# A mixture's first tiles and the attention behind it: routing products, registers, rotary tables and the order of keys

## The chip, the core and the metric

The kernel runs on one core of a Trainium2 chip. A core has five engines with a queue of instructions each: TensorE (PE in the profile, with its weight loads as PEld), VectorE (DVE), ScalarE (ACT), GpSimd (POOL) and SyncE (SP). SP computes nothing; in this kernel it issues most of the transfers between the device memory and the on-chip memory. The metric is the device time of one execution in microseconds, less being better.

## The reference

Four layers, each with an attention and a feed-forward part, on `x` of 4 x 256 tokens with 256 features, and a context of 4 x 1601 tokens. Every part sees a layer norm of `x` and adds its result to `x`. Two parts matter here.

The first feed-forward part is a mixture of eight experts. Each token goes to its two best experts; an expert is three products with biases, with an exact GELU after the first two.

```
gate_weights = softmax(x @ Wg + bg)
topv, topi   = top_k(gate_weights, 2)
h  = gelu(x @ W1[e] + b1[e])
h  = gelu(h @ W2[e] + b2[e])
eo = h @ W3[e] + b3[e]
out = sum over e of comb[.., e] * eo[e]      # comb: topv at topi, 0 elsewhere
```

The attention after it has 16 query heads and 4 heads of keys and values with 128 features. Its keys come from the context and from `x` itself (1601 + 256 = 1857 tokens); queries and keys are normalised by their root mean square and rotated by their positions (cosine and sine of position times frequency).

## The kernel before

The program is one function of some 2,400 lines; its stages follow one another on the one core. A planner of the language sets the order of the instructions within each engine's queue, and places the waits between engines. Inside a block `tc.manual_schedule(engines=...)` the engines named keep the order of the code; the others are still ordered by the planner.

*Routing the first mixture.* The first attention (`topk_attention`) routes three of the four batches beside its own work; the last batch's routing is left as a list of functions, `r["last"]`. It normalises two tiles of `x` (L626 on), multiplies by the gate (L654), finds the two best experts on DVE (L661 to L711), and writes each token's row by an indirect transfer from POOL to a table `XS` in device memory (L727), where each expert has its own range of rows.

*The mixture* (`sparse_moe`, PE, ACT and DVE in the order of the code, POOL and SP by the planner). `more_tiles` turns the counts of tokens into a list of 15 more tiles beyond the first tile of each of the eight experts: for each of the 15 the first row in `XS` and the place of its expert's weights, as whole numbers in `ix`. Whoever addresses memory by these numbers has to load them into registers of its engine (L812, `registers`). In the kernel before, all fifteen are loaded at once on SP (rows), PE and DVE (weights), directly after `ix`, and ahead of the rest:

```
rows = registers(ET.SP, 0, E * ROOM)
at_pe = registers(ET.PE, 1, (E - 1) * 4096)
at_dve = registers(ET.DVE, 1, (E - 1) * 4096)
```

Then come the biases of the 15 tiles (L837, L841: a product and a sum on DVE for each of two layers), and the third layer's biases, which are weighted by `comb` and added to `x` before the tiles (`cT`: transposes L847, copy L848, products L851, `residual` L853 with its sum on L181); `x` then goes to a table `XD` (L854), to which the tiles' results are added. The experts' weights `W` are eight transfers of 2 MB (L801): three at the start, five after the first four row fetches (L824).

The tile loop (L924 on) runs over 23 tiles in a software pipeline. A turn `t` fetches the rows of tile t+4, transposes the rows of tile t+1 (`turn`, L862, L864), does the first product of tile t and the second of tile t-1 (`layer`, L884 with GELU on L891), and the third of tile t-2 (`last`, L903), whose result is scaled (L905) and added to `XD` by an indirect transfer from POOL (L906). For a tile beyond the eighth DVE first copies the expert's weights of the first two layers from a place given by a register (`weights`, L874). The third product reads its weights through a PE register.

Beside the tiles the loop makes the rotary tables of the next attention: `rope_tables` is a generator, and `next(angles, None)` once per turn, from t = 1, does one step. Its first call loads the norm weights `rt_nw` (L953) and multiplies them on DVE (L954). For each of four batches it loads positions (L994), yields, converts them (L997), and does five steps of angles on DVE (L959 to L972), sine on ACT (L1003), products on POOL and DVE (L984 to L988) and a store into the table in device memory (L989). What is left after the loop runs then. At last SP loads `x` back from `XD` (L945).

*The next attention* (`gqa`, PE, ACT, DVE and POOL in the order of the code) gets `layernorm()` of all eight tiles of `x`, done before it starts (statistics L138 and L139, scaling L145, transposes L155). It works in units of one batch and one head of keys. Work is put into numbered slots with phases (`at(slot, phase, function)`). The first unit's queries and keys are made in slots -13 to -5 in ten groups, two a slot: groups 0 and 1 are queries, group 2 the keys of the batch's own `x`, groups 3 to 9 the context's keys. A group takes five slots: product (L1113 or L1187), norm (L1121 or L1194, with powers on POOL at L122) and scaling (L1129 or L1204) in the next one, rotation (L1160 on POOL, L1161 and L1162 on DVE), transposes, copy out. From slot -4 the scores (L1244) run. Weights of a unit come by three transfers (L1058, L1059); the first two units' are issued before the slots. Context and table pieces (`cx`, `tab`) are fetched three slots ahead (L1101, L1104).

Of the kernel before, what the change touches and what calls it, by code (L numbers as in the profile page):

```python
# [12 lines left out]
F32 = mybir.dt.float32  # L13
# [5 lines left out]
P = 128  # L19
B = 4  # L20
# [7 lines left out]
E = 8  # L28
# [24 lines left out]
def kernel(ctx: ExitStack, tc: tile.TileContext, A, out: bass.AP):  # L53
# [730 lines left out]
    def sparse_moe(r, k, XS, XD, tabs):  # L784
        ET = mybir.EngineType
        NT = E + MORE
        with (
# [15 lines left out]

            load(range(3))
            angles = rope_tables(one, tabs)
            for f in r["last"]:
                f()

            ix, ex, oh, _ = more_tiles(one, k, r["cum"], 4096.0)

            def registers(engine, which, top):
                return nc.values_load_multi_w_load_instructions(  # L812
                    ix[0:1, which, :], engines=[engine], min_val=0, max_val=top,
                    skip_runtime_bounds_check_because="made from counts of tokens that add up to twice their number",
                )[1]

            tiles = [{} for _ in range(NT)]

            def place(t, T):
                return T[t * ROOM : t * ROOM + P, :] if t < E else T[bass.ds(rows[t - E], P), :]  # L820

            def fetch(t):
                x = pool.tile([P, ROW], F32, tag="xs", name="xs", bufs=5)
                nc.sync.dma_start(x, place(t, XS))  # L824
                tiles[t]["x"] = x

            for t in range(4):
                fetch(t)
            load(range(3, E))
            rows = registers(ET.SP, 0, E * ROOM)  # L830
            at_pe = registers(ET.PE, 1, (E - 1) * 4096)
            at_dve = registers(ET.DVE, 1, (E - 1) * 4096)
            bias = one.tile([P, 2, MORE, 4], F32, tag="d_b", name="d_b")
            for layer in range(2):
                t4 = pool.tile([P, 1024], F32, tag="wd1024", name="d_t4", bufs=1)[:, 0 : MORE * 4 * E]
                t4 = t4.rearrange("p (d c e) -> p d c e", d=MORE, c=4)
                nc.vector.tensor_tensor(  # L837
                    t4, oh.unsqueeze(2).to_broadcast([P, MORE, 4, E]),
                    b12[:, layer].rearrange("p e c -> p c e").unsqueeze(1).to_broadcast([P, MORE, 4, E]), ALU.mult,
                )  # L840
                nc.vector.tensor_reduce(bias[:, layer], t4, AX.X, ALU.add)  # L841

            for h in range(2):
                cT = one.tile([E, 4 * P], F32, tag="cT", name="cT")
                tr = ps_tr()
                for q in range(4):
                    nc.tensor.transpose(tr[0:E, q * P : (q + 1) * P], r["comb"][:, h * 4 + q, :], ident)  # L847
                nc.scalar.copy(cT, tr[0:E, :])  # L848
                for q in range(4):
                    ps = ps_acc()  # L850
                    nc.tensor.matmul(ps[:, 0:D], cT[:, q * P : (q + 1) * P], b3, start=True, stop=True)  # L851
                    j = h * 4 + q
                    residual(j, ps[:, 0:D])  # L853
                    nc.sync.dma_start(XD[j * P : (j + 1) * P, :], X[j])  # L854

            first = one.tile([P, MORE], F32, tag="d_first", name="d_first")
            nc.vector.tensor_scalar(first, ex, -1.0 / 4096.0, float(E), ALU.mult, ALU.add)
# [9 lines left out]
            def weights(t, n):  # L867

                o, size = ((0, 1024), (1024, 2048))[n]
                if t < E:  # L870
                    w = W[:, t * 4096 + o : t * 4096 + o + size]
                else:
                    w = pool.tile([P, size], F32, tag=f"wd{size}", name=f"wd{size}", bufs=n + 1)
                    nc.vector.tensor_copy(w, W[:, bass.ds(at_dve[t - E] + o, size)])  # L874
                tiles[t]["w", n] = w.rearrange("p (c h) -> p c h", h=512)

            def layer(t, n):
# [15 lines left out]

            def last(t):
                v = tiles[t]
                ps = ps_acc()
                for q in range(4):
                    if t < E:
                        o = t * 4096 + 3072 + q * D
                        w3 = W[:, o : o + D]  # L900
                    else:
                        w3 = W[:, bass.ds(at_pe[t - E] + (3072 + q * D), D)]
                    nc.tensor.matmul(ps[:, 0:D], v["h"][:, q, :], w3, start=(q == 0), stop=(q == 3))  # L903
                y = pool.tile([P, D], F32, tag="y", name="y", bufs=3)
                nc.vector.tensor_scalar(y, ps[:, 0:D], v["g"], 1.0, ALU.mult, ALU.mult)  # L905
                nc.gpsimd.indirect_dma_start(  # L906
                    XD[:, :], bass.IndirectOffsetOnAxis(ap=v["to"], axis=0), y, None, compute_op=ALU.add
                )
# [15 lines left out]
            for t in range(NT + 2):  # L924
                if t + 4 < NT:
                    fetch(t + 4)
                if t + 1 < NT:
                    turn(t + 1)
                if t < NT:
                    layer(t, 0)  # L930
                if t >= 2:
                    last(t - 2)
                if t < NT:
                    weigh(t)
                    weights(t, 1)
                if t + 1 < NT:
                    weights(t + 1, 0)
                if 1 <= t <= NT:
                    layer(t - 1, 1)
                if t >= 1:  # L940
                    next(angles, None)
            for _ in angles:
                pass
            for j in range(NJ):
                nc.sync.dma_start(X[j], XD[j * P : (j + 1) * P, :])  # L945


    def rope_tables(pool, tabs):
# [39 lines left out]
                        nc.vector.scalar_tensor_tensor(tab[:, :, 1, hs], sin[:, 0:m], -1.0, wb[1], ALU.mult, ALU.mult)  # L988
                nc.sync.dma_start(tabs[b][:, at : at + m], tab)  # L989

        waiting = []
        for b in range(B):
            pi = pool.tile([P, nch], I32, tag="pos_i", name="pos_i", bufs=2)
            nc.sync.dma_start(pi, A["pos"][b])  # L994
            pf = pool.tile([P, nch], F32, tag="pos_f", name="pos_f", bufs=2)
            yield
            nc.vector.tensor_copy(pf, pi)  # L997
            for c0 in range(0, nch, 3):
                m = min(3, nch - c0)
                waiting.append((b, c0, m, *angle(b, c0, m, pf)))  # L1000
                yield
                for v in waiting[-1][3:]:
                    nc.scalar.activation(v, v, AF.Sin)  # L1003
                if len(waiting) > 1:
                    products(*waiting.pop(0))
        products(*waiting.pop(0))

    def gqa(xT, key, tabs=None, early=None, others=None):
# [14 lines left out]
        with (  # L1023
# [326 lines left out]

                others(at, lambda b: 4 * (16 * b + 15) + 13)
            weights(0)
            weights(1)
            for u in range(units):
                made = -(-loaded(u) // 2)
                n = len(pairs) - made + 2
                t0 = 16 * (u - 1) - 4 if u else -13
                if made:
                    load_keys(u, t0)
                if u > 1:  # L1360
                    at(t0 - 3, "early", lambda u=u: weights(u))
                for g in range(n):
                    t = t0 + (g // 2 if u == 0 else g * 12 // n)
                    if g < 2:
                        produce_queries(u, g, t)
                    else:
                        produce_keys(u, made + g - 2, t)
# [932 lines left out]
        with rings(0, x=0, tr=3, acc=5):  # L2300
            sparse_moe(r, k, XS, XD, tabs)
    with rings(0, sc0=1, sc1=1, sc2=1, tr=4, acc=1):
        gqa(layernorm(), "l1a", tabs)
    with rings(1):
        linear(layernorm())
    with rings(0, sc=3, tr=1, acc=1):
# [97 lines left out]
```

## Time and profile before

| what | value |
|---|---|
| median of 3 runs | 3754.8 us (3753.04 to 3756.34) |
| the profiled execution's own time | 3761.75 us |
| its span from the first to the last instruction | 3760.0 us |
| TensorE busy, share of the span | 3557.2 us, 95% |
| VectorE, ScalarE, GpSimd busy | 70%, 45%, 35% |
| mean granted TensorE clock | 0.970 |
| first mixture, from the statistics of its last routing to its last product | about 288.7 to 505.1 us |
| first scores of the next attention | 569.35 us |

The profile is one execution, 1.75 us longer than its span and 6.95 us above the median. "PE" rows are matrix products, "PEld" the weight loads that overlap them; rows with a small "q" (SPq, PEldq) are of an engine's sequencer, such as the issue of a transfer or the load of a register. A row of the timeline gives the start, the duration, engine, line, operation, what is written and read, and a count. The chain lists, back from the last instruction, what each step had waited for; "issue" in it is time in which the profile shows no wait. A row of the waits gives who waited, for whom, the total, how often and the longest.

### The profile page before, as it was taken

The page shows a single profiled execution, that of the slowest core. Times are in us where ns is not written, and L with a number is a line of the kernel's source. Part 1 is how long each engine was busy: PE and PEld are TensorE (multiplying, and loading weights), DVE is VectorE, ACT ScalarE, POOL GpSimd, SP SyncE. Part 2 cuts the span into 40 slices and gives each one's busy share as a digit, 9 for nine tenths or more (in the row PEclk, how much of TensorE's full clock was granted, in tenths as well). Part 3 has the DMA queues.
Part 4 walks back from the last instruction along what each step waited for, and adds up shares of the span by engine and source line. Part 5 has one row for each costly group of instructions (what it writes and reads, how often), then busy time and mean ns, then how long its engine had stood idle before and what let it go on. Part 6 is the DMA issues. An engine that isn't in the chain of part 4 may idle for free.

```text
span 3760.0 us, 63083 instructions
## 1 busy us (share of the span) xinstructions
PE 3557.2 (95%) x23397; PEld 2128.8 (57%) x23397; DVE 2615.3 (70%) x5204; ACT 1678.3 (45%) x4926; POOL 1311.5 (35%) x2091
## 2 busy tenths in 40 slices
PE   8887968999999999999999999987999999999998
PEld 4556954555555555555545555553555556556655
DVE  7894856777777777777667676525778766666664
ACT  4442645445444444444224444522444445545532
POOL 3332444444544544444321101012333433333332
PEclk9997989999999999999989999988999999999999
DMA  7326342222221222220100000033111111111103
GB/s 245 102 69 235 85 142 69 63 67 63 73 70 56 59 68 64 65 73 17 40 36 19 1 19 1 1 136 133 42 57 43 57 35 43 56 35 38 28 27 111
DMA packets 173715, 248.50 MB, mean 66 GB/s; under 512 B 21581, under 2 KB 134881, under 8 KB 169825
## 3 DMA queue, kind: packets, MB, share of 16 engines
q1 hardware_dynamic: 167025, 233.00, 19.9%
q0 software_dynamic: 6384, 11.47, 1.4%
q8 instruction: 186, 3.05, 0.3%
q14 instruction: 120, 0.98, 0.1%
HBM read 199.39 MB, written 45.03 MB: 65 GB/s over the span
## 4 chain that ended last, share of the span: by engine, by line
PE 70%; DVE 14%; POOL 7%; issue 5%; ACT 2%; DMA 2%; SPq 0%; another core or an unknown queue 0%; POOLq 0%; DVEq 0%; ACTq 0%
PE acc L1324 17%; PE sc L1244 15%; PE tr L1113 5%; PE sc L1657 4%; PE acc L1676 3%; PE tr L1187 3%; PE sc L1605 3%; DVE PT L1298 3%; POOL pe L1293 3%; PE acc L884 3%; POOL t L1160 2%; PE tr L1553 2%; PE tr L1337 2%; DVE m L521 2%; DVE work L523 1%
## 5 line engine op out<-in xcount | busy, mean ns | idle before, releaser
L1253 ACT ACTIVATE pe<-sc,ms 128x480 f32<-128x480 f32 (+1 forms) x1024 | 643.5, 631 | 892.7 <-DVE ms L1252 862.6
L1324 PE MATMUL acc<-PT,V 128*128 128x256 f32 (+1 forms) x3584 | 895.9, 390 | 6.9 <-ACT OT L1331 6.9
L1244 PE MATMUL sc<-KT,QT 128*32 128x480 f32 (+5 forms) x8192 | 883.1, 535 | 15.4 <-ACT pe L1253 12.1
L1293 POOL TENSOR_SCALAR pe<-pe,fac 128x480 f32<-128x480 f32 (+1 forms) x1024 | 654.8, 659 | 586.2 <-ACT pe L1253 213.7
L1324 PEld LDWEIGHTS acc<-PT,V 128*128 128x128 f32 (+1 forms) x3584 | 641.8, 190 | 349.4 <-issue 206.5
L1252 DVE TENSOR_REDUCE ms<-sc 128x1 f32<-128x480 f32 (+1 forms) x1024 | 607.9, 615 | 139.9 <-PE sc L1244 119.9
L1298 DVE STREAM_TRANSPOSE PT<-pe 128x1920 f32<-128x1920 f32 (+1 forms) x256 | 519.5, 2030 | 0.0
L1244 PEld LDWEIGHTS sc<-KT,QT 128*32 128x32 f32 x8192 | 220.9, 109 | 402.1 <-issue 321.8
L122 POOL TENSOR_TENSOR rs<-rsq_t,mhalf 128x2 f32<-128x2 f32 (+2 forms) x248 | 160.2, 646 | 568.6 <-DVE rsq_t L121 563.9
L1663 ACT ACTIVATE pt<-sc 128x1024 f32<-128x1024 f32 (+1 forms) x224 | 215.5, 962 | 280.7 <-PE sc L1657 245.9
L1113 PE MATMUL tr<-w,cx 128*128 128x256 f32 (+1 forms) x1264 | 303.5, 382 | 1.3 <-ACT nk L1129 1.3
L1619 DVE TENSOR_REDUCE mx<-sc 128x2 f32<-128x982 f32 (+2 forms) x224 | 211.6, 957 | 98.9 <-PE sc L1605 65.8
L1113 PEld LDWEIGHTS tr<-w,cx 128*128 128x128 f32 (+1 forms) x1264 | 226.7, 187 | 31.6 <-ACT nk L1129 2.0
L1657 PE MATMUL sc<-QT,KT 32*128 32x256 f32 (+1 forms) x1664 | 240.4, 403 | 0.0
L1605 PE MATMUL sc<-KT,QT 32*128 32x491 f32 (+4 forms) x1024 | 236.9, 564 | 0.0
L1253 ACT ACTIVATION_READ_ACCUMULATOR pe<-sc,ms 128x1 f32 x1024 | 199.4, 195 | 0.0
L1657 PEld LDWEIGHTS sc<-QT,KT 32*128 32x128 f32 (+1 forms) x1664 | 139.2, 182 | 92.8 <-issue 72.9
L1121 ACT ACTIVATE sq<-tr 128x128 f32<-128x128 f32 (+1 forms) x348 | 96.8, 278 | 171.5 <-PE tr L1113 166.4
L122 POOL TENSOR_TENSOR rsq<-rsq_t,mhalf 128x4 f32<-128x4 f32 x64 | 65.2, 1018 | 308.5 <-DVE rsq_t L121 308.5
L1676 PE MATMUL acc<-pt,vbuf 128*32 128x256 f32 (+1 forms) x1792 | 142.5, 391 | 0.0
L1161 DVE TENSOR_TENSOR nk<-nk,tab 128x256 f32<-128x256 f32 (+1 forms) x128 | 65.6, 513 | 100.2 <-POOL t L1160 99.0
L1187 PE MATMUL tr<-w,xlnT 128*128 128x512 f32 x256 | 126.1, 618 | 3.8 <-DMA wo<-in_l1a_wo 3.1
(430 smaller groups left out, 4774.5 us busy)
## 6 DMA issues: line engine op xcount, KB each, us to landing
cx<-in_ctxT SPq DMA_DIRECT2D x144, 256.0 KB, 3.0
tab<-rope SPq DMA_DIRECT2D x112, 256.0 KB, 2.7
w<-in_l0f_w SPq DMA_DIRECT2D x8, 2048.0 KB, 19.8
ctxT<-in_ctxT SPq DMA_DIRECT2D x7, 1601.0 KB, 6.5
w<-in_l2f_w SPq DMA_DIRECT2D x8, 1088.0 KB, 8.2
w<-in_l1a_wq SPq DMA_DIRECT2D x16, 512.0 KB
wo<-in_l1a_wo SPq DMA_DIRECT2D x16, 512.0 KB, 4.8
w<-in_l3a_wq SPq DMA_DIRECT2D x16, 512.0 KB, 7.3
```

The lines of the kernel that those rows point to most:

```text
L122: nc.gpsimd.tensor_tensor(dst, t[:n, :k], mhalf[:n, :k], ALU.pow)
L1113: nc.tensor.matmul(v["ps"][:n, i, :], lhs, st["wkv"][:, c, :], start=(c == 0), stop=(c == NC_ - 1))
L1187: nc.tensor.matmul(v["ps"], xtok(xT, b * 2 + tt, c), state[u]["wq"][:, c, :], start=(c == 0), stop=(c == NC_ - 1))
L1244: nc.tensor.matmul(sc[32 * r : 32 * r + 32, 0 : lens[r]], st["QT"][:, tt, o : o + 32], st["KT"][:, r, 0 : lens[r]], start=True, stop=True,)
L1252: nc.vector.tensor_reduce(top, sc, AX.X, ALU.max, negate=True)
L1253: nc.scalar.activation(w, sc, AF.Exp, bias=top, accum_out=s)
L1293: nc.gpsimd.tensor_scalar(w, w, v["fac"][:, g * 4 + a : g * 4 + a + 1], 1.0, ALU.mult, ALU.mult)
L1298: nc.vector.transpose(state[steps[i]][:, :, g * P : (g + 1) * P].rearrange("p k (a t) -> p a k t", a=4), pes[g].rearrange("p a (k i) -> p ...
L1324: nc.tensor.matmul(v["ps"][:, 0 : 2 * P], V[:n, k, :], PT[:n, k, :], start=(k == 0), stop=(k == nch - 1))
L1605: nc.tensor.matmul(st[:, j, c : c + n], QT[r, g, tt * P : (tt + 1) * P], KT[r, g, o : o + n], start=True, stop=True,)
L1657: nc.tensor.matmul(st[:n, j, q, :], KT[r, g, o : o + n], QT[r, :], start=True, stop=True)
L1676: nc.tensor.matmul(acc[32 * j : 32 * j + 32, a, :], V[:n, place, h * VW : h * VW + 32], pt[:n, j, q, :], start=(k == 0), stop=(k == nch - ...
```

## The change

In the mixture:

- `next(angles)` is called once ahead of `r["last"]`. The generator now loads all four position tiles, each into a buffer of its own, before its first yield, and does not yield again for each batch; twenty angle steps and the rest after the last one remain for the loop.
- Registers are loaded one by one: on SP where a tile's rows are fetched, on DVE where a tile's weights are first copied, on PE for tiles 8 to 15 ahead of the loop and for the others in `last`.
- The third layer's biases (`cT`) come directly after `more_tiles`; the first four row fetches stand after their first half, the last five weight transfers after their second half.
- The biases of the 15 tiles become a function that is called in turns 2 and 3.
- `x` is loaded back by transfers that ACT issues, no longer SP.

In the next attention:

- The layer norm is not finished before: its four pairs of tiles are put into slots, the first at -13 to -11, the others from -9, -8 and -7 on.
- The ten groups of the first unit come in the order 3, 4, 5, 6, 0, 1, 2, 7, 8, 9.
- The second unit's weights are issued in slot -12.

```diff
             load(range(3))
             angles = rope_tables(one, tabs)
+            next(angles)
             for f in r["last"]:
                 f()
 
             ix, ex, oh, _ = more_tiles(one, k, r["cum"], 4096.0)
 
-            def registers(engine, which, top):
+            def register(engine, which, i, top):
                 return nc.values_load_multi_w_load_instructions(
-                    ix[0:1, which, :], engines=[engine], min_val=0, max_val=top,
+                    ix[0:1, which, i : i + 1], engines=[engine], min_val=0, max_val=top,
...
             def place(t, T):
-                return T[t * ROOM : t * ROOM + P, :] if t < E else T[bass.ds(rows[t - E], P), :]
+                if t < E:
+                    return T[t * ROOM : t * ROOM + P, :]
+                return T[bass.ds(register(ET.SP, 0, t - E, E * ROOM), P), :]
...
-            for t in range(4):
-                fetch(t)
-            load(range(3, E))
-            rows = registers(ET.SP, 0, E * ROOM)
-            at_pe = registers(ET.PE, 1, (E - 1) * 4096)
-            at_dve = registers(ET.DVE, 1, (E - 1) * 4096)
-            bias = one.tile([P, 2, MORE, 4], F32, tag="d_b", name="d_b")
-            for layer in range(2):
...
                     residual(j, ps[:, 0:D])
                     nc.sync.dma_start(XD[j * P : (j + 1) * P, :], X[j])
+                if h == 0:
+                    for t in range(4):
+                        fetch(t)
+            load(range(3, E))
+            for t in range(E, E + 8):
+                tiles[t]["pe"] = register(ET.PE, 1, t - E, (E - 1) * 4096)
+            bias = one.tile([P, 2, MORE, 4], F32, tag="d_b", name="d_b")
+
+            def biases(layer):
...
-                    nc.vector.tensor_copy(w, W[:, bass.ds(at_dve[t - E] + o, size)])
+                    if n == 0:
+                        tiles[t]["dve"] = register(ET.DVE, 1, t - E, (E - 1) * 4096)
+                    nc.vector.tensor_copy(w, W[:, bass.ds(tiles[t]["dve"] + o, size)])
...
                 v = tiles[t]
+                if t >= E + 8:
+                    v["pe"] = register(ET.PE, 1, t - E, (E - 1) * 4096)
...
+                if t in (2, 3):
+                    biases(t - 2)
                 if t >= 1:
                     next(angles, None)
             for _ in angles:
                 pass
             for j in range(NJ):
-                nc.sync.dma_start(X[j], XD[j * P : (j + 1) * P, :])
+                nc.scalar.dma_start(X[j], XD[j * P : (j + 1) * P, :])
...
-        waiting = []
+        waiting, where = [], []
         for b in range(B):
-            pi = pool.tile([P, nch], I32, tag="pos_i", name="pos_i", bufs=2)
-            nc.sync.dma_start(pi, A["pos"][b])
+            where.append(pool.tile([P, nch], I32, tag=f"pos{b}", name="pos", bufs=1))
+            nc.sync.dma_start(where[b], A["pos"][b])
+        yield
+        for b in range(B):
             pf = pool.tile([P, nch], F32, tag="pos_f", name="pos_f", bufs=2)
-            yield
-            nc.vector.tensor_copy(pf, pi)
+            nc.vector.tensor_copy(pf, where[b])
...
             weights(0)
-            weights(1)
+            at(-12, "early", lambda: weights(1))
...
-                for g in range(n):
-                    t = t0 + (g // 2 if u == 0 else g * 12 // n)
+
+                order = [3, 4, 5, 6, 0, 1, 2, *range(7, n)] if rope and u == 0 else range(n)
+                for x, g in enumerate(order):
+                    t = t0 + (x // 2 if u == 0 else x * 12 // n)
...
-        gqa(layernorm(), "l1a", tabs)
+        xT, pairs = normed()
+
+        def norms(at, done):
+            for p, t in zip(pairs, (-13, -9, -8, -7)):
+                for f, slot, phase in zip(p, (t, t + 1, t + 2), ("early" if t == -13 else "late", "pe", "early")):
+                    at(slot, phase, f)
+
+        gqa(xT, "l1a", tabs, others=norms)
```

## The prediction

> **What bounds the kernel now.** First the page: TensorE (PE) fills the span as a whole, so a gain has to come from a stretch where it does not.
>
> ```profile
> span 3760.0 us, 63083 instructions
> PE 3557.2 (95%) x23397; PEld 2128.8 (57%) x23397; DVE 2615.3 (70%) x5204; ACT 1678.3 (45%) x4926; POOL 1311.5 (35%) x2091
> ```
>
> Then the chain in order of time, from 270 to 400 us and from 470 to 660 us. The diff touches two such stretches: the head of the first mixture, and the way from it into the next attention.
>
> ```profile
> 299.10 0.43 PE acc L742 x2
> 299.53 9.31 issue
> 308.84 1.02 PE tr L847 x4
> ...
> 314.80 25.98 DMA xd<-x
> ...
> 341.76 3.16 DMA rt_nw<-in_l1a_nw
> ...
> 345.56 3.68 PE acc L884 x16
> ```
> ```profile
> 519.26 2.29 DMA rope<-rt
> ...
> 523.01 5.51 DMA wo<-in_l1a_wo
> 528.55 6.05 PE tr L1187 x8
> ...
> 569.35 3.52 PE sc L1244 x13
> ```
>
> Then the waits of 293 to 350 us (who, for whom, total, times, longest): PE's two gaps at the head, and VectorE (DVE) held by one small load.
>
> ```profile
> PE tr L847 <- issue: 9.3, 1, 9.3
> PE tr L862 <- DMA xs<-xs: 5.9, 1, 5.9
> ```
> ```profile
> DVE rt_nw L954 <- DMA rt_nw<-in_l1a_nw: 19.0, 1, 19.0
> ```
>
> The DMA queue's own waits and SyncE's (SP's) rows say why: stores behind the 2 MB weight pieces wait up to 4.9 us for each piece.
>
> ```profile
> SPq L854 <- DMA w<-in_l0f_w: 22.6, 5, 4.9
> ```
> ```profile
> 288.65 0.33 SPq L797 DMA_DIRECT2D b<-in_l0f_b  x1
> 288.67 0.43 DVE L626 BATCH_NORM_STATS2 bnst<-x 128x6 f32<-128x256 f32 x1
> 289.02 1.29 SPq L801 DMA_DIRECT2D w<-in_l0f_w  x3
> ```
>
> Last, what a register load costs: fifteen at once 4.3 us on PE (the 9.3 gap ends with it), one alone 0.30.
>
> ```profile
> L2184 PEldq TENSOR_LOAD <-d_ix x15: 296/301/446, 3698.6 to 3720.9; - x15
> L812 PEldq TENSOR_LOAD <-d_ix x1: 4272/4272/4272, 304.5 to 304.5; - x1
> ```
>
> **The change part by part.** Times are against this execution (3761.75 us for a span of 3760.0; it lies 6.95 above the median of the runs, 3754.8). + is later.
>
> *Head.* (a) `next(angles)` now stands ahead of the last batch's routing, and it does more than issue loads: it multiplies `rt_nw` on DVE (L954), and DVE keeps program order, as the 19.0 us wait shows. Its load comes after three weight pieces on SP. The pieces, issued at 289.02, land about 4.9 us apart (the trace has 296.7, 301.6, 307.2; the last was slowed by row scatters), so the load behind them lands near 307. Its consumer then takes 0.23, and the statistics start at 307.3 instead of 288.67: **+18.6** on everything up to the tiles (routing, scatters, expert products). The four position loads are small and wait for nobody. (b) The products of L847 and L851 no longer wait for registers: the gap of **-9.3** goes. Late next are the residuals on DVE, which follow the routing arithmetic within the products' 10.9 us. (c) Eight single loads before the first tile: 8 x 0.30 = **+2.4** on PE (0 if its sequencer runs ahead, as the later mixture's rows do; I take all). DVE's fifteen ran beside PE's and go; fifteen single ones of 0.28 lie under the 1.2 us copy before each. The seven other PE loads lie under matmuls, as those of L2184 do, and SP's fifteen (0.28 each, four tiles ahead) under 7.3 us tiles: 0, or at worst 7 x 0.3 = 2.1 exposed. Tile 0 thus moves from 319.70 to 331.4. (d) The second stall: `turn(4)` could have run at 337.84 and the next tile at 345.15 (later transposes of L862 start 7.31 apart); it ran at 354.37, for rows behind weights, DVE held by `rt_nw`, and a clock of 0.5 afterwards. With SP idle for 18 us more, the remaining five pieces, which wait for no data, should be brought ahead, as the planner brought three position loads ahead at 342 to 347. Then rows of tile 4 are there when PE wants them (349.5): **-9.2**. Sum here +2.5.
>
> *Tile loop.* The twenty angle steps move from tiles 2 to 24, with four pauses, to tiles 1 to 20 without one; thirteen lie on tiles with weight copies in both. DVE is then nearly full: bursts of five end with periods of 7.91, 7.50 and 7.48 against 7.31. Without pauses I add **+1.2** (0 to 5). The biases (2 x 1.64 on DVE at tiles 2 and 3) lie beside 7.3 us of PE, where DVE is busy 4 to 5.7; without that cover +3.3. In the last tiles ACT no longer swaps tables for Sin (1.28 each) before Gelu: from the last `turn` at 480.67 PE took 24.4 us, of which 22.3 are work and Gelu waits: **-2.1**. PE ends at 506.7 instead of 505.09: +1.6.
>
> *Into the attention.* The `X` loads need the last indirect add (landed 510.14, 5.05 after PE's end) in either version. Now ACT issues them. No row shows an ACT issue; by SP's (0.32 to 0.49) eight take 2.6 to 3.9 us, which lie before ACT's first square; uncovered +3.9. On SP they leave ahead of the weights. (e) The weights (L1058) waited for the last rope store and left at 521.70, 16.6 after PE's end. The stores end with tile 21 now; next late is that same add, 5.05 after PE's end (511.75): **-11.55**. (f) PE then waited 6.85 for the query weights. Now its first work wants `wkv` and the first `cx`, the fourth load on SP; before, the fourth landed 8.4 after the first issue and the sixth 11.4, and 1 MB of `X` now comes in at the same time. I take 10: **+3.15** (+1.5 to +4.5). (g) From PE's start to the first scores took 40.8, a chain through in-order engines, POOL's rotations first. Keys reach their first rotation about 2.1 sooner than the 12.4 of the queries (512-wide squares, 1.0 us powers), and the query projections (6.04 at half clock) run 1.2 shorter. But three normalisations that were done before now stand among them: two statistics 0.43, two 0.18, 0.15, a 0.7 wait for POOL, 0.74 of scaling, so 2.85 each, 8.5: **+5.2** (-3.3 if they hide, DVE being busy 6.65 of the last 14 us; +8.5 if nothing is saved). `weights(1)` goes behind the first fetches and is wanted nine slots later: 0.
>
> Sum: 18.6 - 9.3 + 2.4 - 9.2 + 1.2 - 2.1 = +1.6 at PE's end, and -11.55 + 3.15 + 5.2 = -3.2 from there to the first scores (569.35 becomes 567.75). After them the same code runs in the same order, so the end moves as the scores do: **-1.6**, and 3754.8 - 1.6 = 3753.
>
> The Trainium skill has a rule that speaks against moving the `X` loads ("DMA: Bandwidth & Descriptors", section "Issuing engines are not separate DMA queues"): transfers started by different engines run on the same 16 DMA engines, and a second issuer saves only issue time. The row beside it is the 2.1 us landing of the first `X` load on an otherwise quiet queue. By the rule (f) would be near its upper end, +4.5, and without it near +1.5; no run here shows an ACT-issued load yet.
>
> **The rivals.**
> 1. *The small load is not behind the weights*, because the planner puts `rt_nw` first. For: it reorders ready loads elsewhere. Against: here SP kept the order of the code, and everything waited for one event (L469). Then -18.6, but the tile-4 rows are behind five pieces (landed 340.4, stores 1 MB less: 338.6), so the stall stays in part: turn(5) at 347.8 instead of 354.37, -6.6 where I have +2.5. -1.6 - 9.1 = -10.7: 3744.
> 2. *The slower side: the five pieces stay behind the first rows.* In before, W7 landed 31.8 us after the first row fetch was issued (308.56 to 340.36). From 327.2 that is 359 to 360, so `turn(4)` comes at 360.2 instead of 349.5, with 1.9 of slow clock: up to +12. -1.6 + 12: 3765. It decides (slower by 0.2%) once the rows come after about 357. For: that was the order before. Against: SP then had no idle time to fill by the planner's account, now it has.
> 3. *The normalisations hide* in DVE's idle time: (g) -3.3 instead of +5.2: 3745.
>
> **How the numbers follow.** 0.2%, about 7.5 us, is what a measurement of this kernel can tell from no change. Forecast 0.52 (3753, own range 3745 to 3761; 0.06 of it faster, 0.05 slower); rival 1 0.14 (0.11 faster); rival 2 0.21 (0.17 slower); rival 3 0.13 (0.09 faster). Together faster 0.26, same 0.52, slower 0.22. The range runs from between rivals 1 and 3 to a little over rival 2: 3741 to 3767.
>
> **What would show it.** (a) DVE L954 waits about 18 us for its load near 289, and the last statistics start near 307. (b) No 9 us gap before the expert products. (d) No wait for rows at tile 4. Weights of the attention issued about 5 us after the mixture's last matmul, and the first PE work on `cx`. (g) first scores about 61 us after that matmul. Wrong if DVE does not wait at (a), if PE waits over 3 us at tile 4, or if scores start under 55 us after the mixture.

## The result, and the profile after

The changed kernel takes 3765.12 us (median of 9 runs, 3759.86 to 3770.99) against 3754.8 for the kernel before beside it: a ratio of 1.0026, 95% interval 1.0017 to 1.0034. It is slower by a quarter of a per cent. The forecast was 3753, the same time or a little less; the time lies inside the range, where the rival "the five pieces stay behind the first rows" had put it.

The profiled execution of the changed kernel took 3766.08 us for a span of 3764.3. Its page begins as that of before does:

```profile
span 3764.3 us, 63125 instructions
PE 3551.9 (94%) x23397; PEld 2127.2 (57%) x23397; DVE 2617.8 (70%) x5204; ACT 1686.6 (45%) x4931; POOL 1315.3 (35%) x2091
```

PE does the same work in 3551.9 us instead of 3557.2 and still ends later: it waits more. Where, the chain of waits in order of time (start, us, what) shows, first at the head of the mixture, then on the way into the attention:

```profile
282.47 27.85 issue
...
328.08 3.79 PE acc L839 x8
331.89 0.42 DVE x L181
332.79 0.38 SPq L842
333.23 0.45 SPq L801
333.72 0.45 SPq L801
334.21 0.43 SPq L801
334.69 17.56 DMA xs<-xs
352.38 0.41 PE tr L867 x2
```
```profile
513.23 0.49 DVE y L914
513.99 3.77 DMA xd<-y,y_to
518.40 0.61 SPq L1070
519.06 6.57 DMA w<-in_l1a_wq
525.64 0.55 SPq L1113
526.24 3.76 DMA tab<-rope
530.19 3.77 PE tr L1125 x8
```

The first line, 27.85 us without a wait on record, spans a wait of VectorE. The waits between 285 and 360 us (who, for whom, total, times, longest) name it, and the tile 4 wait that is left:

```profile
DVE rt_nw L965 <- DMA pos<-in_pos: 20.1, 1, 20.1
...
PE tr L867 <- DMA xs<-xs: 2.7, 1, 2.7
```

The row names the position loads, which SP issued directly behind the load of `rt_nw`. In the trace `rt_nw` itself, issued at 290.90, landed at 309.09, and the multiplication ran at 309.31; all of these small loads stood behind the three pieces, the last of which landed at 307.08.

SP's rows of the same stretch (start, us, what) show the order of the issues: two pieces (L801) after the position loads, then nothing until the stores and the row fetches, then the three other pieces, and the rows of tile 4 behind them.

```profile
289.56 1.29 SPq L801 DMA_DIRECT2D w<-in_l0f_w  x3
290.90 0.64 SPq L964 DMA_DIRECT2D rt_nw<-in_l1a_nw  x1
291.58 2.03 SPq L1005 DMA_DIRECT2D pos<-in_pos  x4
297.30 5.23 SPq L801 DMA_DIRECT2D w<-in_l0f_w  x2
...
329.51 1.76 SPq L827 DMA_DIRECT2D xs<-xs  x4
331.36 1.81 SPq L842 DMA_DIRECT2D xd<-x  x4
333.23 1.42 SPq L801 DMA_DIRECT2D w<-in_l0f_w  x3
334.69 24.65 SPq L827 DMA_DIRECT2D xs<-xs  x5
```

The positions in the two profiled executions, in us from the start of the span:

| | before | forecast | after |
|---|---|---|---|
| last statistics | 288.67 | 307.3 | 310.19 |
| tile 0, first transposes | 319.71 | 331.4 | 332.22 |
| turn(5) | 354.37 | 356.9 | 361.36 |
| PE's end of the mixture | 505.09 | 506.7 | 513.21 |
| weights of the attention, after that end | 16.6 | 5.05 | 5.2 |
| PE's first projection, after that end | 23.5 | 15.05 | 17.0 |
| first scores, after that end | 64.3 | 61.05 | 64.8 |

### The profile page after: what moved, and what is told of

Same layout as the page of the kernel before. It is cut to its first block, busy times and chain, and to the rows that moved or that the text cites. A ratio compares the mean times of both kernels' runs of the same rounds, so it can differ in the third digit from the quotient of the medians.

```text
span 3764.3 us, 63125 instructions
## 1 busy us (share of the span) xinstructions
PE 3551.9 (94%) x23397; PEld 2127.2 (57%) x23397; DVE 2617.8 (70%) x5204; ACT 1686.6 (45%) x4931; POOL 1315.3 (35%) x2091
## 4 chain that ended last, share of the span: by engine, by line
PE 67%; DVE 14%; POOL 8%; issue 6%; DMA 3%; ACT 2%; SPq 1%; POOLq 0%; DVEq 0%; ACTq 0%
PE acc L1336 16%; PE sc L1256 15%; PE tr L1125 5%; PE sc L1671 4%; PE acc L1690 3%; POOL pe L1305 3%; DVE PT L1310 3%; PE tr L1199 3%; PE sc L1619 3%; POOL t L1172 2%; PE tr L1567 2%; PE acc L891 2%; PE tr L1349 2%; DVE m L521 2%; DVE work L523 1%
## 5 line engine op out<-in xcount | busy, mean ns | idle before, releaser
L1125 PE MATMUL tr<-w,cx 128*128 128x256 f32 (+1 forms) x1264 | 304.3, 383 | 18.3 <-DMA tab<-rope 17.0
L1633 DVE TENSOR_REDUCE mx<-sc 128x2 f32<-128x982 f32 (+2 forms) x224 | 211.6, 957 | 94.7 <-PE sc L1619 61.7
L1125 PEld LDWEIGHTS tr<-w,cx 128*128 128x128 f32 (+1 forms) x1264 | 227.2, 187 | 48.9 <-issue 17.4
```

Source lines behind the costliest of these rows:

```text
L1125: nc.tensor.matmul(v["ps"][:n, i, :], lhs, st["wkv"][:, c, :], start=(c == 0), stop=(c == NC_ - 1))
```

## The experiments

All times are medians, each with that of the kernel before in the same session; differences are taken against that one, because it moved between 3754.8 and 3756.7. Positions are from each kernel's one profiled execution. "From PE's end" runs from the mixture's last product to the first scores.

| kernel | time | before beside it | ratio (95%) | tile 0 | turn(5) | PE's end | from PE's end |
|---|---|---|---|---|---|---|---|
| after | 3765.1 | 3754.8 | 1.0026 (1.0017–1.0034) | 332.2 | 361.4 | 513.2 | 64.8 |
| e1_nw_late | 3758.5 | 3755.3 | 1.0009 (1.0000–1.0018) | 312.9 | 354.3 | 508.4 | 64.6 |
| e2_pieces_first | 3767.4 | 3755.3 | 1.0031 (1.0019–1.0043) | 339.3 | 364.5 | 520.5 | 63.7 |
| e3_old_attention | 3764.2 | 3755.3 | 1.0023 (1.0014–1.0032) | 333.8 | 362.9 | 517.2 | 62.2 |
| e4_new_attention | 3764.4 | 3755.3 | 1.0025 (1.0015–1.0034) | 321.5 | 356.1 | 507.5 | 72.1 |
| e5_x_on_sp | 3766.8 | 3756.7 | 1.0031 (1.0019–1.0044) | 330.0 | 358.9 | 512.8 | 64.7 |
| e6_norms_first | 3762.9 | 3756.7 | 1.0022 (1.0013–1.0031) | 332.7 | 361.8 | 516.1 | 63.2 |
| e7_rows_ahead | 3748.3 | 3756.7 | 0.9979 (0.9970–0.9988) | 312.6 | 338.1 | 495.5 | 64.9 |
| e8_old_order_w1 | 3762.3 | 3756.7 | 1.0017 (1.0008–1.0026) | 333.3 | 362.1 | 513.0 | 61.7 |
| e9_angles_later | 3742.6 | 3756.0 | 0.9964 (0.9952–0.9976) | 313.8 | 339.5 | 492.2 | 64.4 |
| e10_together | 3739.2 | 3756.0 | 0.9959 (0.9945–0.9973) | 311.4 | 336.9 | 492.6 | 62.9 |
| e11_before_rows | 3753.0 | 3756.0 | 0.9992 (0.9983–1.0001) | 319.1 | 355.7 | 506.3 | 59.4 |
| e12_wq_later | 3760.2 | 3756.0 | 1.0012 (1.0003–1.0021) | 332.0 | 361.4 | 514.1 | 60.3 |
| e13_two_undone | 3754.7 | 3756.7 | 0.9992 (0.9983–1.0001) | 312.3 | 353.6 | 507.9 | 60.4 |
| e14_best | 3739.6 | 3756.7 | 0.9952 (0.9939–0.9966) | 312.7 | 338.4 | 494.5 | 62.8 |
| e15_registers_only | 3754.8 | 3756.7 | 0.9997 (0.9988–1.0006) | 312.8 | 354.4 | 504.9 | 63.7 |

### The head of the mixture

**The multiplication of `rt_nw`, moved behind the loads.**

```
-        nc.vector.tensor_scalar_mul(nw[:, 0, :], nw[:, 0, :], HD**-0.5)
 ...
             nc.sync.dma_start(where[b], A["pos"][b])
         yield
+        nc.vector.tensor_scalar_mul(nw[:, 0, :], nw[:, 0, :], HD**-0.5)
```

> The changed kernel with one instruction moved: VectorE multiplies rt_nw when the first angle step runs (tile 1), not ahead of the last batch's routing; the loads stay early. Theory (the wait for the small load sets the head): the last statistics start near 289 us instead of 309.5 and turn(0) near 312 instead of 332.2. Then the rows of tile 4 are late behind the pieces (near 342), so that turn(5) comes at 348 to 352 instead of 361.4, and the time is 9 to 13 us under the changed kernel's: 3752 to 3756. Rival (the wait is only moved, because turn(4) goes with the pieces' landing and these stay where they are): turn(5) at 358 to 361, time 3762 to 3765.

Tile 0 comes 19.4 us sooner, turn(5) 7.1, the time is 7.1 nearer to the kernel before (+3.2 instead of +10.3; at 3758.5 it misses the 3752 to 3756 of the theory, and the rival's 3762 too). So the one instruction carries most of the slowdown. But of its 19.4 us only 7 count; PE's transposes say why (start, us, idle before):

```profile
312.87 1.19 PE L867 MATMUL tr<-ident,xs 128*128 128x128 f32 x4 [1.87 <-DMA xs<-xs]
...
344.05 0.66 PE L867 MATMUL tr<-ident,xs 128*128 128x128 f32 x2 [12.51 <-DMA xs<-xs]
...
354.30 0.38 PE L867 MATMUL tr<-ident,xs 128*128 128x128 f32 x2
```

The early start runs into a wait of 12.5 us for the rows of tile 4, which the trace has behind the five pieces (landed 343.9; the last piece 343.6). turn(5) then stands where it stood in the kernel before. The expected 348 to 352 was too early, as the pieces landed 5.3 us apart here.

**The register and bias edits alone**, on the kernel before (diff: the parts of the change at `register`, `place`, `biases`, `weights`, `last` and the place of the fetches; rotary tables, `X` loads and attention left as they were).

> The kernel before with the register and bias edits alone (the prediction's parts (b) and (c), biases' sums at tiles 2 and 3): rotary tables, X loads and attention as before. Theory ((b) is a true gain of 6.9 us at tile 0, which the rows behind the pieces and VectorE's wait for rt_nw take back): turn(0) at 312 to 313, turn(5) at 352 to 355 as before (354.37), time 3753 to 3757. Rival (the earlier start carries through): turn(5) at 347 to 349, time 3747 to 3750.

Tile 0 at 312.78 instead of 319.71: the 6.9 us booked for (b) and (c) are there, though not from the terms that were booked (point 2 below). turn(5) at 354.39 instead of 354.37: nothing of it is left, and the time is the same. The first row is tile 0; at tile 4 the wait has only changed its size:

```profile
312.78 1.16 PE L866 MATMUL tr<-ident,xs 128*128 128x128 f32 x4 [1.61 <-DMA xs<-xs]
...
343.37 0.66 PE L866 MATMUL tr<-ident,xs 128*128 128x128 f32 x2 [11.91 <-DMA xs<-xs]
...
354.39 0.38 PE L866 MATMUL tr<-ident,xs 128*128 128x128 f32 x2
```

**All pieces ahead, as step (d) took for granted.**

```
             next(angles)
+            load(range(3, E))
             for f in r["last"]:
 ...
-            load(range(3, E))
```

> The changed kernel with the five later weight pieces issued directly after the position loads, ahead of the last batch's routing (what the prediction's step (d) took for granted). Theory: the rows of tile 4 are there before PE wants them, the stall of 2.7 us and the slow clock after it (1.7) go: turn(5) near 357 instead of 361.4, time 4 to 5 under the changed kernel's (3760 to 3761). Rival 1 (as the prediction had it): turn(5) at 356.9, the same by another way. Rival 2: the pieces hold up the last row scatters and the first row fetches, so that turn(0) slips by as much as is gained or more: 3765 to 3775.

Rival 2 holds. The wait at tile 4 is gone (turn(4) to turn(5) 7.31), but tile 0 comes 7.1 later: the row scatters from POOL, issued beside the pieces, take 7.4 to 9.2 us to land in this trace, against 2.4 to 3.0 in the changed kernel's, and the first row fetches wait for them.

```profile
298.64 12.78 SPq L801 DMA_DIRECT2D w<-in_l0f_w  x5
...
337.22 1.76 SPq L828 DMA_DIRECT2D xs<-xs  x4
```
```profile
339.29 1.37 PE L867 MATMUL tr<-ident,xs 128*128 128x128 f32 x4 [5.92 <-DMA xs<-xs]
```

So step (d) was wrong twice: the order did not come, and it would not have brought the gain.

**Rows of tiles 4 and 5 ahead of the pieces**, first on the kernel before alone, then together with the late multiplication:

```
-                x = pool.tile([P, ROW], F32, tag="xs", name="xs", bufs=5)
+                x = pool.tile([P, ROW], F32, tag="xs", name="xs", bufs=6)
 ...
-            for t in range(4):
+            for t in range(6):
                 fetch(t)
 ...
-                if t + 4 < NT:
+                if 6 <= t + 4 < NT:
                     fetch(t + 4)
```

> The kernel before with one thing changed: the rows of tiles 4 and 5 fetched with the first four, ahead of the five pieces (one buffer more). It asks what ended the second stall there (turn(5) at 354.37): the rows behind the pieces, or VectorE, held by the rt_nw multiplication until 341.8. Theory (both): VectorE still stands until 341.8, turn(5) at 349 to 352, time 2 to 5 under the time before: 3751 to 3754. Rival (the rows alone, as the prediction's step (d) had it): turn(5) at 345 to 346, time 8 to 9 under it: 3746 to 3748.

> The changed kernel with the rt_nw multiplication at tile 1 (as in the run before: turn(0) at 312.9, turn(5) at 354.3, 3758.5 us) and the rows of tiles 4 and 5 fetched with the first four, ahead of the five later weight pieces (one buffer more). Theory (behind the small load, the second wait is for those rows behind the pieces, and nothing else stands there): no wait at tile 4, turn(5) at 339 to 342, time 12 to 15 under that run: 3743 to 3747. Rival 1 (the pieces themselves come next: tiles 3 to 7 wait for their weights): turn(5) at 346 to 352, 3750 to 3756. Rival 2 (the early start lets the clock or another stage give the time back): turn(5) at 340, but the time at 3752 or more.

In the kernel before it brings nothing at turn(5) (355.69, where the theory had 349 to 352). Two waits stood one behind the other there, and with the rows gone VectorE's remains, first in its own waits, then in PE's:

```profile
DVE rt_nw L954 <- DMA rt_nw<-in_l1a_nw: 19.6, 1, 19.6
```
```profile
PE acc L884 <- DVE xsT L864: 8.2, 1, 8.2
```

(The 3 us by which this kernel's median is lower, with an interval that still reaches 1.0001, come later: SP issued the query weights at 517.65, ahead of the last rope store and not behind it, and the scores follow PE's end by 59.4.) With both waits gone, turn(5) is at 338.1, 16.2 earlier than with the late multiplication alone, and the time 8.4 under the kernel before (3748.3, where the theory had 3743 to 3747). It gained 11.6, though, not 16: the tile loop gave some back (157.4 us from turn(5) to PE's end instead of 154.1).

**Angles from tile 3 on.** `if t >= 1:` ahead of `next(angles, None)` becomes `if t >= 3:`, on top of the last kernel.

> The run with the rows ahead of the pieces (3748.3 us, turn(5) at 338.1, PE's end at 495.5), with the angle steps from tile 3 on instead of tile 1. In that run the tile loop gave time back: 157.4 us from turn(5) to PE's end, against 150.7 before and 151.8 in the changed kernel, with one period of 10.7; there VectorE stood for 5.7 us at a product whose buffer waited for a rope store, and that store had landed 10.4 us after its issue, behind the weight pieces. Theory: the first products come after the last piece, that wait goes, 153 to 155 from turn(5) to PE's end, PE's end at 491.5 to 493, time 3744 to 3746. Rival 1 (VectorE is full in the tiles with weight copies whenever the steps run): still 156 to 158, time 3747 to 3750. Rival 2 (the steps now end at tile 22, Sin and Gelu swap tables in the last tiles and the rope stores hold the attention's weights): 155 to 156, and PE's end to scores 66 or more, 3748 to 3752.

From turn(5) to PE's end 152.7 instead of 157.4, and 13.4 under the kernel before instead of 8.4: the theory holds, a little better than expected. In the kernel without this edit the wait read

```profile
DVE rt L998 <- ACT ang_r L1015: 5.6, 1, 5.6
...
PE acc L891 <- DVE xsT L869: 3.2, 1, 3.2
```

and names ScalarE, but VectorE went on at 348.50, and the rope store that frees the buffer of L998 landed at 348.4 in the trace. That the store ended it is read from this, and agrees with the gain.

### The way into the attention

**The attention's part undone, and done alone.** One kernel is the change with `gqa(layernorm(), "l1a", tabs)`, `order = range(n)` and `weights(1)` as before; the other is the kernel before with the new lines of these three places.

> The changed mixture with the attention as it was before (queries first, all normalisations ahead, second unit's weights directly behind the first's). Theory (the new order costs more than it saves: PE's first work 11.8 instead of 6.85 after the weights, and 47.8 instead of 40.8 from there to the first scores): the weights still come 5.2 after PE's end, PE starts some 7 to 9 after them, scores 41 later, so 54 to 56 from PE's end to the first scores instead of 64.8: 9 to 11 under the changed kernel's time, 3754 to 3756. Rival (the X loads and the shared DMA engines set it, not the order): scores 62 to 65 after PE's end, 3762 to 3765.

> The kernel before with only the attention's part of the change (keys of the context first, three normalisations among them, second unit's weights later). Theory: weights as before at 521.7, PE's first work 9 to 12 after instead of 6.85, first scores 46 to 48 after that instead of 40.8: scores at 577 to 581 instead of 569.35, 8 to 12 over the time before: 3763 to 3767. Rival (what was slow in the changed kernel came from the X loads on ACT's queue): PE's first work 7 to 8 after the weights, normalisations hidden: 3753 to 3758.

Alone, the new order costs what the theory said (+7.9 to the scores, +9.1 in time). Undone, it brings little: 62.2 instead of 64.8, and +8.9 instead of +10.3; here the rival was right. Weights that come 11 us sooner than in the kernel before brought the scores only 2.0 nearer to PE's end; the chain suggests why, as everything else is fetched at the same time. The old order's first queries came 22.0 after PE's end (23.5 before), and its chain shows a rotary table that left behind two units' weights:

```profile
522.99 7.33 DMA w<-in_l1a_wq
...
532.22 0.43 SPq L1192
532.69 6.46 DMA tabq<-rope
539.18 2.05 PE tr L1199 x2
```

**Old order, with the second unit's weights late** (as above, but `at(-12, "early", lambda: weights(1))` kept).

> The changed mixture with the attention's old order (queries first, all normalisations ahead), but the second unit's weights after the first fetches, as in the change. Where the second unit's weights followed the first's directly, PE's first query work came 22 us after PE's end, held by a rotary table that landed behind them, and the first scores 62.2 after. Theory (those 0.75 MB stood in the way): query work 16 to 18 after PE's end, scores 56 to 59 after it, time 3757 to 3761. Rival (X and the normalisations set the start): scores 61 to 64, time 3762 to 3765.

61.7: at the rival's lower end, and again only some of the gain; first queries at 20.6. X and its normalisations arrive no sooner.

**The `X` loads on SP**: `nc.scalar.dma_start(X[j], ...)` becomes `nc.sync.dma_start`.

> The changed kernel with the eight X loads issued by SyncE again, ahead of the attention's weights, instead of by ScalarE beside them. Theory (what comes after PE's end is 1 MB of X and the weights, which share the transfers whoever issues them): the weights are issued some 3.5 us later, X lands some 4 to 8 us sooner, and PE's end to the first scores stays at 63 to 67 us (64.8 in the changed kernel): time within 3 us of the changed kernel's 3765. Rival (the shared queue of issues cost the 11.8 us between weights and first work): PE's first work 8 to 9 after the weights, 61 to 63 to the first scores, 2 to 4 faster. Other rival (weights first is worth it): 68 or more.

64.7 and +10.1: it makes no difference who issues. This is what the Trainium skill states ("DMA: Bandwidth & Descriptors", section "Issuing engines are not separate DMA queues"): transfers of several issuers share the same 16 engines, and only issue time is saved. Weights were issued 3.4 us later, and the first keys came at 18.3 instead of 17.0.

**All normalisations ahead, new order kept**: `gqa(layernorm(), "l1a", tabs)` in place of `norms`.

> The changed kernel with all four normalisations ahead of the attention again, the rest of the new order (context keys first, second unit's weights later) kept. Prices the prediction's step (g). Theory (three normalisations in the chain cost 5 us, as the prediction summed): first scores 58 to 61 us after PE's end instead of 64.8, time 3759 to 3762. Rival (the X tiles' arrival, 12 to 15 us after PE's end, then holds VectorE and PE in program order ahead of the first keys): 65 to 70, time 3765 to 3770.

PE now does the transposes of `X` first, and the keys' products (L1125) come after them:

```profile
529.82 1.08 PE L155 MATMUL tr<-ident,xl 128*128 128x128 f32 x4 [13.68 <-DVE xl L145]
533.05 1.11 PE L155 MATMUL tr<-ident,xl 128*128 128x128 f32 x4 [2.15 <-DVE xl L145]
...
538.24 1.19 PE L1125 MATMUL tr<-w,cx 128*128 128x256 f32 x2 [0.37 <-DMA tab<-rope]
```

From the first keys to the scores 41.1 instead of 47.8, so the normalisations in the chain cost 6.7. (Step (g) had 8.5 for them, less 3.3 that the new order was to save. The 41.1, against 40.8 in the old order before, shows no such saving.) But the keys start 5.1 later, and the net is 1.6: between theory and rival.

**Query and output weights after the first fetches.**

```
-                for t, n in ((wkv, "_wkv"), (wq, "_wq")):
-                    nc.sync.dma_start(t, A[key + n] ...)
-                nc.sync.dma_start(wo, ...)
+                def rest():
+                    nc.sync.dma_start(wq, ...)
+                    nc.sync.dma_start(wo, ...)
+                nc.sync.dma_start(wkv, ...)
+                if late:
+                    at(-15, "early", rest)
+                else:
+                    rest()
 ...
-            weights(0)
+            weights(0, rope)
```

> The changed kernel, with the first unit's query and output weights (1 MB) issued after the first fetches of context and tables instead of ahead of them, so that the first keys wait for the key weights, one context piece and one table alone (the prediction's step (f): PE's first work 10 after the weights; measured 11.8, 17.0 after PE's end). Theory (those transfers stood in the way): first keys 12.5 to 14.5 after PE's end, scores 61 to 63 after it instead of 64.8, time 3761 to 3763. Rival (the chain behind, queries and normalisations, sets the scores): first keys earlier, scores 64 to 66, time 3764 to 3767.

More than expected: first keys 10.8 after PE's end instead of 17.0, scores 60.3 instead of 64.8, and +4.2 in time instead of +10.3. SP's rows and PE's first work:

```profile
519.12 0.61 SPq L1073 DMA_DIRECT2D w<-in_l1a_wkv  x1
519.78 0.60 SPq L1119 DMA_DIRECT2D cx<-in_ctxT  x1
520.42 0.61 SPq L1122 DMA_DIRECT2D tab<-rope  x1
...
524.75 0.54 SPq L1070 DMA_DIRECT2D w<-in_l1a_wq  x1
```
```profile
524.92 6.25 PE L1131 MATMUL tr<-w,cx 128*128 128x256 f32 x16 [10.80 <-DMA x<-xd]
```

So what the context-first order lacked was its transfers in the same order: the keys went first on PE, and 1 MB of query and output weights went ahead of their context on SP. Two things changed here at once, and no run separates them fully: the 1 MB ahead of the first context piece, and a stand of SP before it issued that piece (12.4 us after PE's end in the changed kernel, 5.7 here). With the `X` loads on SP the piece left at 10.6, and still landed no sooner (17.4 after PE's end against 16.4), which speaks for the transfers ahead and not for the stand.

### Together

**Both repairs in the changed kernel**: the late multiplication, and the query and output weights after the first fetches.

> The changed kernel with two things put right together: the rt_nw multiplication at tile 1 (alone it took back 6.7 us) and the first unit's query and output weights after the first fetches (alone 5.0). Theory (the two waits are what made the change slower): they add, turn(5) near 354, PE's end near 508, scores 60 to 61 later, time 3752 to 3755, no slower than the kernel before. Rival (a third cause in the tile loop or later): 3756 to 3760, PE's end to the end of the span unchanged but 154 or more from turn(5) to PE's end.

They nearly add. Alone they took back 7.1 and 6.1 of the 10.3 us, together 12.3; the kernel is then level with the one before (ratio 0.9992, interval 0.9983 to 1.0001). No third cause is needed, though the tile loop's share (point 4 below) is within what this can miss.

**The fastest mixture with either attention**: old order with late second weights, or new order with late query weights.

> The same (small load's consumer late, rows ahead, angles from tile 3), with the attention's old order: queries first, all normalisations ahead, second unit's weights after the first fetches (in the changed mixture: 61.7 us from PE's end to the scores instead of 64.8, 2.8 us of time). Theory: the parts add: PE's end at 491.5 to 493, scores 61 to 63 later, time 3740 to 3744, some 11 to 16 under the kernel before. Rival (the parts share a cause): 3745 to 3749, no better than with the rows ahead alone.

> The fastest mixture so far (3742.6 us: late multiplication, rows of tiles 4 and 5 ahead, angles from tile 3; 64.4 from PE's end to the scores) with the first unit's query and output weights after the first fetches (alone: 64.8 became 60.3, 5.0 us of time). Theory: these add, scores near 60 to 61 after PE's end, time 3737 to 3740. Rival (the angles end two tiles later here, so that the rope stores come beside the first loads and take the gain): 64 to 66, 3742 to 3745.

3739.2 and 3739.6, 16.8 and 17.1 us under the kernel before beside them (0.9959 and 0.9952), better than both kernels of this study. The last parts did not add fully: 62.9 and 62.8 from PE's end to the scores instead of 61.7 and 60.3. The angles end two tiles later here. In both traces POOL makes the last rotary products ahead of the last indirect add, which so leaves 2.55 us after PE's end and not 0.8, and the weights, which follow its landing, leave at 6.5 and not at 5.1. In the second kernel the loop also took 156.1 us from turn(5) to PE's end instead of 152.7. So the late angles cost here, as the rival of the second kernel had it, but through POOL's order and at a smaller size; what part is chance of one profiled execution stays open.

## Why the prediction was wrong, point by point

From the median before to the median after the forecast was -1.6, and +10.3 was measured: 11.9 us of error.

1. **(a), the right wait, 2.9 us too small.** VectorE stood for 20.1 us, and the last statistics moved by 21.5 where 18.6 was booked. The small load landed 2.0 after the third piece, not with it. And both statistics of the batch now stand behind it (309.45 and 310.19), where the kernel before had done the first at 270.65; the prediction counted only the second. The price of the one instruction at tile 0 is 19.4.
2. **(b) and (c), the sum right by luck.** -6.9 booked, -6.9 measured at tile 0 when done alone. But (c) came out at 0 and not at +2.4: the eight loads lie under the last expert products. In the run alone a wait that no term had stands in its place, 1.61 us for the rows of tile 0. In the changed kernel PE hardly waited before tile 0:

```profile
332.22 1.09 PE L867 MATMUL tr<-ident,xs 128*128 128x128 f32 x4 [0.37 <-issue]
```

There the two gave about 9.0, an estimate from two positions: the routing's last products (L742) moved by 21.5 us, tile 0 by 12.5. So tile 0 at 332.22, close to the 331.4 forecast, is (a) booked too low and (b) with (c) booked too high.
3. **(d) is the step that failed, 4.5 us.** "The remaining five pieces should be brought ahead": two were, three stayed behind the row fetches though SP issued nothing from 302.5 to 326.0 (why the planner stopped at two, the runs do not show), and turn(5) moved by +7.0 instead of +2.5. It was rival 2's mechanism in a milder form (a wait of 2.7 at tile 4 and then a period of 9.0). The deeper fault is that the sum added (a) to (d) at tile 0, while the rows behind the pieces set turn(5): with that bound in place (b) and (c) are worth 0 there, and (a) 7.1.
4. **Tile loop and tail, 2.0 us.** From turn(5) to PE's end +1.1 in this pair (151.8 against 150.7) where -0.9 was forecast. It is rather more: five other executions of the same loop took 150.9 to 154.3, mean of all six 153.0, while the loop with before's angle steps took 150.6 to 151.3 in four. PE's own waits for the weight copies on VectorE, between 355 and 520 us in the kernel before and in the changed one, show a part of it:

```profile
PE acc L884 <- DVE wd L874: 0.8, 2, 0.5
```
```profile
PE acc L891 <- DVE wd L881: 2.5, 3, 1.2
```

That VectorE is full there, with thirteen tiles of angles and weight copies and no pause, fits this but was not tested by itself. The tail (from the last `turn` to PE's end) brought 0.7 of the 2.1.
5. **(e), right, and worth little.** Weights 5.2 after PE's end (5.05). **(f), 1.8 short**: first work 11.8 after the weights, not 10. That is 4.9 more than before, over the upper end of its range (+4.5), and the late query weights showed why. **(g), 1.8 short**: 47.8 against 46.0. The normalisations cost 6.7, less than the 8.5 booked, but the 3.3 that the new order was to save did not come. Together 0.5 lost instead of 3.2 won, 3.7 us.
6. The last 1.7 us (8.6 at the scores, 10.3 by the medians) are not traced. A part may be the loop: with the +2.2 that the means of point 4 give in place of +1.1, 0.6 would be left, as an estimate. The spans of the two profiled executions differ by 4.3 alone; the one before lies 7 above its median, and took 3190.6 us from its first scores to its end where the sixteen other kernels' executions took 3181.8 to 3187.4.

The rivals: "not behind the weights" fell with (a); "normalisations hide" fell with the 6.7 that they cost; "the pieces stay behind the first rows" was the mechanism; it priced turn(4) at up to +12 where turn(5) came out 4.5 later than forecast, and the rest of its 3765 was made up by points 4 to 6, which were no part of it. That its number was met is luck. It had a chance of 0.21.

## What to carry to other kernels

A gain ahead of a stage counts only up to the next wait in it: ask what ends that wait (here the rows behind 10 MB of weights), and price the edit there, not where it is made. When an order of computing changes, change the order of the transfers with it. A generator's first step that loads and computes should load alone: a consumer in program order ahead of other work waits for whatever queue the load is on.

## What the runs showed of the hardware

- Bulk transfers slow small ones of another issuer as well: a row scatter from POOL landed after 2.4 to 3.0 us in the changed kernel, where no piece was on its way, and after 7.4 to 9.2 beside the 2 MB pieces in the run with all pieces ahead.
- SP and ACT drew their completion semaphores for transfers from the same eight in turn, in this program. With ACT's eight `X` loads between, SP's fourth issue after PE's end stood until the query weights of two issues before had landed (issue at 525.64, landing at 525.63 in the changed kernel). A second issuer so brought a wait to the first one.
- A wait of PE costs more than its length. In the windows of the changed kernel and of the one with the late multiplication (us, busy time of each engine, then the granted clock) the tile after the wait runs at 0.81 after 2.7 us of waiting and at 0.70 after 12.5: 8.98 and 10.25 us instead of 7.31. In the five other runs that wait 2.3 to 3.2 us there (e3, e5, e6, e8 and e12 of the table) the tile takes 8.96 to 9.00.

```profile
352.40:361.30 8.90, 8.90 (x58) 8.50 (x59) 3.56 (x10) 2.83 (x7) 4.52 (x7) 0.81 0.13 20
361.40:370.00 8.60, 8.60 (x72) 8.39 (x70) 7.20 (x26) 6.54 (x16) 3.26 (x4) 1.00 0.56 161
```
```profile
344.10:354.20 10.10, 10.10 (x58) 9.57 (x59) 3.52 (x10) 2.42 (x5) 1.59 (x1) 0.70 0.10 17
```
